# Scores of a 32-head attention laid out with tokens on partitions, one head at a time in two column tiles

## The chip, the cores and the metric

The kernel runs on one core of a Trainium2 chip. The metric is the device time of one execution in microseconds (us); less is better. Five engines work beside each other, each through its own queue of instructions in order: TensorE (PE, matmuls and their weight loads), VectorE (DVE), ScalarE (ACT), GpSimd (POOL) and SyncE (SP, which issues DMAs). They wait for each other by semaphores. Tensors live in SBUF (128 partitions) and matmul results in PSUM banks.

## The reference, cut to what matters

The reference is a decoder of four layers on `x` of 16 x 64 tokens by 512, each an attention with a context and a feed-forward part. The change touches the attention of the second layer only: 32 query heads, 8 key/value heads, head size 128, queries and keys normalised by their root mean square. Every sequence has 64 context tokens and 64 stream tokens, so 128 keys.

```python
kv = jnp.concatenate([context, latents], axis=1)
q = (latents @ Wq).reshape(bsz, q_len, HEADS, HEAD_DIM).transpose(0, 2, 1, 3)
...
q = rms_norm(q, q_norm_w)
k = rms_norm(k, k_norm_w)
qg = q.reshape(bsz, KV_HEADS, groups, q_len, HEAD_DIM)
scale = 1.0 / np.sqrt(HEAD_DIM)
scores = jnp.einsum('bhgqd,bhkd->bhgqk', qg, k) * scale
probs = jax.nn.softmax(scores.astype(jnp.float32), axis=-1).astype(q.dtype)
out = jnp.einsum('bhgqk,bhkd->bhgqd', probs, v)
```

The factor that `rms_norm` gives a query is one number for each token and head. It can be multiplied into the query, or into that query's row of scores later.

## The kernel before

All arithmetic of this attention is fp32. The 1024 tokens are eight tiles of 128 (two sequences of 64 each). A unit is one key/value head with its four query heads (G = 4) on one token tile: 8 heads x 8 tiles = 64 units, two tiles at a time.

Two lanes of work share the core. Lane a runs this attention (`normed_attention`); beside it lane b runs the first layer (window attention with VectorE products, an int8 feed-forward), and then the later parts for half of the tokens. `merged` writes one order of instructions from both by hand: each step of lane a yields a cost, and lane b advances until its own costs have used that up. For PE that order is kept as written (`manual_schedule`, line 1680); the order on the other engines is left to the framework. Each lane has four PSUM banks that it takes in rotation.

Inside lane a `ticks` (line 206) runs the units as a software pipeline. In each tick, in this order: `scores` of the unit begun two ticks ago, `scale` of one tick ago, `project` of five, `queries` of this one, `turn` of one ago, `keys_values` of this one, `values` of four, `turn_weights` of three.

The steps of one unit, with the lines that matter:

- `queries` (838): loads of the context's keys and values from DRAM, the query product (line 857) into a bank, squares into `sq` (865), a copy to SBUF as `qn` (867); tokens are on the partitions, the four heads side by side.
- `keys_values` (870): key and value product (875), square of the keys (883), copies; then `factors`: one sum over `sq` for four query heads and the key (798), a small scaling (799) and a power of -1/2 on POOL (123) give `r`, 128 x 5.
- `scale` (893): DVE multiplies `qn` by its four factors (898, 128 x 512) and `kn` by the fifth (899, 128 x 128), placed behind the latest maximum on DVE's queue (`issue_after(at.last)`).
- `turn` (901): PE transposes the four query blocks (line 141, `ps_qT`), ACT copies them to `qT` with the sequence ahead of the head (905); PE transposes the keys (`ps_kT`) and ACT writes them with the norm weights `nqk` as its scale (909).
- `scores` (914) calls `Attention.weights` (666), which the last layer uses too: four matmuls, each with the 64 tokens of two heads as 128 stationary columns against the 128 keys of their sequence (672). Partitions are therefore (head, token) pairs, and the four blocks are two sequences by two pairs of heads. DVE takes the row maxima (682) and scales them (683); ACT takes four exponentials with the maximum as bias and sums the rows as it goes (688); DVE inverts the sums (696), and POOL multiplies (697).
- `turn_weights` (919): four transposes on PE (`ps_pT`), copied by DVE to `pT` (704).
- `values` (923): two matmuls, values stationary, 256 columns of `pT` moving (713); ACT copies to `aT` (927).
- `project` (930): four matmuls of 512 columns (722), and the residual add on DVE (157).

On PE the score block mostly stands between the transposes `ps_pT` and the projection `ps_wo`. Two other places have blocks of 128 rows by 64 stationary columns: the values' projection of the third layer's attention (line 1110, its last tile) and this attention's context keys (line 809).

Of the kernel before, what the change touches and what calls it, by code (L numbers as in the profile page):

```python
# [8 lines left out]
F32 = mybir.dt.float32  # L9
# [4 lines left out]
AF = mybir.ActivationFunctionType  # L14
ALU = mybir.AluOpType
AX = mybir.AxisListType

P = 128
B, S, D = 16, 64, 512
NTOK = B * S  # L20
NT = NTOK // P
NC = D // P
# [7 lines left out]
def bc(ap, axis, n):  # L30

    a = ap.unsqueeze(axis)
    shape = list(a.shape)
    shape[axis] = n
    return a.to_broadcast(shape)
# [14 lines left out]
VECTOR = mybir.EngineType.DVE  # L50
# [605 lines left out]
class Attention:  # L656


    G = 4
# [6 lines left out]
    def weights(self, qT, kTs):  # L666
# [30 lines left out]
        nc.gpsimd.tensor_tensor(p, p, bc(sm, 2, P), ALU.mult)  # L697
        return p

    def turned(self, p):  # L700

        ps = self.ln.transposed(p.rearrange("p i n -> p (i n)"), 4, "ps_pT")
        pT = self.pool.tile([P, 2, 2 * P], F32, tag="pT", name="pT")
        self.nc.vector.tensor_copy(  # L704
            pT.rearrange("p b n -> p (b n)"), ps.rearrange("p i n -> p (i n)")
        )
        return pT
# [20 lines left out]
def normed_attention(ln, groups, rates, w_in, w_kv, norms):  # L728
# [5 lines left out]
    k, nc = ln.k, ln.nc  # L734
    HD, NKV = 128, 8
    with ExitStack() as es:
        wpool = ln.pool(es, "l1w")
        pool = ln.pool(es, "l1a")
        at = Attention(ln, pool, HD)
        G = at.G  # L740
        nw = pool.tile([P, 2], F32, tag="nw", name="nw", bufs=1)
        nc.sync.dma_start(nw, norms)

        nqk = pool.tile([P, 1], F32, tag="nqk", name="nqk", bufs=1)
        nc.vector.tensor_tensor(nqk, nw[:, 0:1], nw[:, 1:2], ALU.mult)
        NQ, NKVW = NC * G * HD, NC * 2 * HD
        w_qkv, w_o, kept = {}, {}, {}

        def qkv_weights(n):
            if n < NKV * len(groups) and n not in w_qkv:  # L750
                w = wpool.tile([P, NQ + NKVW], F32, tag="qkv", name=f"l1a_w{n}")
                nc.sync.dma_start(w, w_in[n % NKV, :, : NQ + NKVW])
                w_qkv[n] = (
                    w[:, :NQ].rearrange("p (c n) -> p c n", c=NC),
                    w[:, NQ:].rearrange("p (c n) -> p c n", c=NC),
                )

        def out_weights(n):
            if n >= 0 and n not in w_o:
                w = wpool.tile([P, G * D], F32, tag="o", name=f"l1a_o{n}")  # L760
                nc.sync.dma_start(w, w_in[n % NKV, :, NQ + NKVW :])
                w_o[n] = w.rearrange("p (g n) -> p g n", g=G)

        def queries(u):
            n, t = u
            if t == groups[n // NKV][0]:
                qkv_weights(n)
                qkv_weights(n + 1)
                out_weights(n - 2)
            ps = ln.bank([P, G, HD], "ps_q")  # L770
            for c in range(NC):
                nc.tensor.matmul(
                    ps,
                    lhsT=k.stream(c, t),
                    rhs=w_qkv[n][0][:, c, :],
                    start=c == 0,
                    stop=c == NC - 1,
                )
            sq = pool.tile([P, 6, HD], F32, tag="sq", name="sq", bufs=1)
            nc.scalar.activation(sq[:, 0:4, :], ps, AF.Square)  # L780
            qn = pool.tile([P, G, HD], F32, tag="qn", name="qn")
            nc.scalar.copy(qn, ps)
            kept[u] = dict(sq=sq, qn=qn)

        dram = es.enter_context(
            ln.tc.tile_pool(name="saved", bufs=1, space=bass.MemoryType.DRAM)
# [106 lines left out]
        def scale(u):  # L893

            d = kept[u]
            qn, kn, r = d["qn"], d["kn"], d.pop("r")
            with ln.tc.issue_after(at.last) if at.last is not None else ExitStack():
                nc.vector.tensor_tensor(qn, qn, bc(r[:, 0:G], 2, HD), ALU.mult)
                nc.vector.tensor_scalar_mul(kn, kn, r[:, G : G + 1])

        def turn(u):
            d = kept[u]
            ps = ln.transposed(d.pop("qn").rearrange("p g d -> p (g d)"), G, "ps_qT")
            qT = pool.tile([P, 2, G, S], F32, tag="qT", name="qT")
            nc.scalar.copy(
                qT.rearrange("p b g s -> p g b s"), ps.rearrange("p g (b s) -> p g b s", b=2)
            )
            ps = ln.transposed(d.pop("kn"), 1, "ps_kT")
            nc.scalar.mul(
                d["kT"][:, 1:3, :], ps.rearrange("p c (b s) -> p (c b) s", b=2), nqk  # L910
            )
            d["qT"] = qT

        def scores(u):
            d = kept[u]
            kT = d.pop("kT")
            d["p"] = at.weights(d.pop("qT"), [kT[:, 1 - j : 4 - j : 2, :] for j in range(2)])

        def turn_weights(u):
            d = kept[u]  # L920
# [1 line left out]

        def values(u):
            d = kept[u]
            ps = at.values(d.pop("pT"), d.pop("v"))
            aT = pool.tile([P, G, 2, S], F32, tag="aT", name="aT")
            nc.scalar.copy(aT.rearrange("p g b s -> p b g s"), ps)  # L927
            d["aT"] = aT

        def project(u):  # L930
# [13 lines left out]
            [(NKV * i + h, t) for i, ts in enumerate(groups) for h in range(NKV) for t in ts],  # L944
            [
                (2, scores, 0.9),
                (1, scale, 0.0),
                (5, project, 3.4),
                (0, queries, 3.4),
                (1, turn, 0.7),  # L950
                (0, keys_values, 1.7),
                (4, values, 0.9),
                (3, turn_weights, 0.4),
            ],
# [650 lines left out]
def decoder_kernel(ctx: ExitStack, tc: tile.TileContext, i: dict, out: bass.AP):  # L1605
# [64 lines left out]
    def main():  # L1670
        yield Need(0, 1.0)
        yield from normed_attention(
            a, groups, [0.85, 0.78, 0.78, 0.74], i["l1a_w"], i["l1a_kv"], i["l1a_n"]
        )
        yield Need(len(groups) + 2, 1.0)
        a.pages(ctx)
        yield from mxfp4_ffn(a, halves[1], None, i["l1f_b"], kept_w)
        yield from last_layers(a, halves[1])
# [92 lines left out]
```

## Time and profile before

| what | value |
|---|---|
| median of 3 runs | 1642.59 us (1637.8 to 1644.62) |
| span of the profiled execution | 1642.0 us, 0.6 below that median |
| granted TensorE clock, mean | 0.993 |
| score matmuls of the 64 units (line 672, 128 x 128) | 512 records, 275 ns each, 67.8 us of PE busy |
| weight loads of these | 512 records, 192 ns each |
| multiply of the queries by their factors (line 898) | 64 x 683 ns on DVE |
| exponentials (line 688, all callers) | 384 x 369 ns on ACT |
| transposed queries' copy (line 905) | 64 x 604 ns on ACT |

The profiled execution's time is its span, from the first instruction to the last; it is near the median of the runs, so sums made against the span hold for the runs. In the views below a group of instructions is named by line, engine, operation and "out<-in", with tile shapes; "128*64 128x128" is a matmul with 128 rows by 64 columns of weights and a moving operand of 128 partitions by 128 elements. A matmul's record lasts longer than it holds PE, since matmuls are pipelined; what one costs is read from the start of one record to the start of the next. PEld are the weight loads, which overlap matmuls.

### The profile page before, as it was taken

How to read it: one execution, taken by the hardware profiler on the slowest of the kernel's cores; microseconds unless marked ns; L12 is line 12 of the kernel's file. 1: busy time of each engine (PE TensorE's matmuls, PEld its weight loads, DVE VectorE, ACT ScalarE, POOL GpSimd, SP SyncE). 2: the span in 40 equal slices, each digit the busy share in tenths (PEclk: the TensorE clock that was granted, in tenths of full speed). 3: DMA queues.
4: the chain of work that ended last, by engine and by line, in shares of the span. 5: the costliest groups of instructions: out<-in, count | busy, mean ns of one | idle time of the engine just before them, and what ended most of it. 6: DMA issues, size and time to landing. Idle time of an engine off the chain costs nothing.

```text
span 1642.0 us, 20849 instructions
## 1 busy us (share of the span) xinstructions
PE 1590.8 (97%) x7104; PEld 918.9 (56%) x7104; DVE 962.6 (59%) x2000; ACT 614.7 (37%) x1929; POOL 506.2 (31%) x523
## 2 busy tenths in 40 slices
PE   7999899899999999999999999999999999999999
PEld 1334456465555645666655565554566566556774
DVE  6686588566687567776964365338246333522335
ACT  3333354334443444434443454221244332223442
POOL 1493238522385313853322132012022101011112
PEclk9999999999999999999999999999999999999999
DMA  8982359523693346943633222022220101301120
GB/s 259 272 261 82 109 164 257 177 87 120 190 279 118 109 139 176 271 162 107 231 119 126 102 74 97 29 109 73 72 71 20 46 20 49 96 29 42 39 71 26
DMA packets 98329, 200.32 MB, mean 122 GB/s; under 512 B 48945, under 2 KB 66097, under 8 KB 86449
## 3 DMA queue, kind: packets, MB, share of 16 engines
q1 hardware_dynamic: 98224, 199.00, 39.1%
q8 instruction: 57, 0.93, 0.2%
q14 instruction: 48, 0.39, 0.1%
HBM read 179.57 MB, written 19.40 MB: 121 GB/s over the span
## 4 chain that ended last, share of the span: by engine, by line
PE 80%; DVE 10%; DMA 4%; ACT 3%; POOL 2%; issue 1%; SPq 0%; ACTq 0%; POOLq 0%; DVEq 0%
PE ps_wo L722 15%; PE ps_q L857 10%; PE ps_ckv L809 7%; PE ps_kv L875 5%; PE ps_q L1462 5%; PE ps_s L672 4%; PE ps_a L713 4%; PE ps_o L1313 3%; PE ps_h L1288 3%; PE ps_pT L141 3%; DMA att<-att_d 3%; PE ps_v L1409 3%; PE ps_k L1446 2%; PE ps_dot L390 2%; PE ps_wo L1203 2%; PE ps_q L1135 2%
## 5 line engine op out<-in xcount | busy, mean ns | idle before, releaser
L722 PE MATMUL ps_wo<-l1a_o,aT 128*128 128x512 f32 x512 | 231.1, 594 | 3.1 <-ACT aT L927 3.1
L857 PE MATMUL ps_q<-l1a_w,kvT 128*128 128x512 f32 x512 | 233.0, 598 | 0.0
L688 ACT ACTIVATE p<-ps_s,mx 128x128 f32<-128x128 f32 x384 | 135.4, 369 | 211.2 <-DVE mx L683 192.4
L697 POOL TENSOR_TENSOR p<-p,sm 128x512 f32<-128x512 f32 x96 | 103.7, 1080 | 337.3 <-DVE sm L696 303.0
L123 POOL TENSOR_TENSOR r<-r,mhalf 128x5 f32<-128x5 f32 (+1 forms) x96 | 102.9, 1072 | 294.6 <-DVE r L799 280.4
L857 PEld LDWEIGHTS ps_q<-l1a_w,kvT 128*128 128x128 f32 x512 | 96.4, 192 | 117.5 <-issue 116.1
L722 PEld LDWEIGHTS ps_wo<-l1a_o,aT 128*128 128x128 f32 x512 | 92.7, 190 | 100.8 <-issue 96.3
L157 DVE TENSOR_TENSOR x<-x,ps_wo 128x512 f32<-128x512 f32 x104 | 70.6, 679 | 115.2 <-PE ps_wo L722 83.0
L875 PE MATMUL ps_kv<-l1a_w,kvT 128*128 128x256 f32 x512 | 125.0, 388 | 1.1 <-DVE x L157 0.9
L476 POOL TENSOR_TENSOR acc<-acc,pv 128x512 f32<-128x512 f32 x96 | 122.0, 1295 | 4.7 <-DVE pv L466 4.0
L809 PE MATMUL ps_ckv<-l1a_kv,kvT 128*64 128x512 f32 x512 | 116.9, 599 | 0.0
L798 DVE TENSOR_REDUCE r<-sq 128x5 f32<-128x640 f32 x64 | 52.3, 817 | 109.9 <-ACT sq L883 109.9
L123 POOL TENSOR_TENSOR rs<-rs,mhalf 128x1 f32<-128x1 f32 x64 | 36.7, 578 | 259.1 <-DVE rs L132 225.1
L875 PEld LDWEIGHTS ps_kv<-l1a_w,kvT 128*128 128x128 f32 x512 | 94.2, 194 | 18.6 <-issue 4.2
L865 ACT ACTIVATE sq<-ps_q 128x512 f32<-128x512 f32 x64 | 38.2, 597 | 158.3 <-PE ps_q L857 158.2
L466 DVE TENSOR_TENSOR pv<-att,ps_v 128x512 f32<-128x512 f32 x128 | 82.1, 676 | 22.1 <-DMA att<-att_d 18.8
L672 PE MATMUL ps_s<-kT,qT 128*128 128x128 f32 (+1 forms) x704 | 92.1, 276 | 0.1
L369 DVE TENSOR_TENSOR prod<-qs,kp 128x1024 f32<-128x1024 f32 x64 | 79.0, 1272 | 15.4 <-ACT qs L350 7.4
L704 DVE COPY pT<-ps_pT 128x512 f32<-128x512 f32 x96 | 64.3, 683 | 39.3 <-PE ps_pT L141 39.2
L672 PEld LDWEIGHTS ps_s<-kT,qT 128*128 128x128 f32 (+1 forms) x704 | 85.0, 192 | 3.4 <-issue 2.1
L1462 PE MATMUL ps_q<-kvT,l3a_w 128*128 128x256 f32 x384 | 85.6, 379 | 0.0
L722 PE MATMUL ps_wo<-l3a_o,aP 128*128 128x512 f32 x192 | 85.5, 593 | 0.0
(193 smaller groups left out, 2720.8 us busy)
## 6 DMA issues: line engine op xcount, KB each, us to landing
l1a_w<-in_l1a_w SPq DMA_DIRECT2D x32, 1536.0 KB, 7.0
att<-att_d SPq DMA_DIRECT2D x64, 512.0 KB, 9.2
l1a_o<-in_l1a_w SPq DMA_DIRECT2D x32, 1024.0 KB, 5.2
s<-ckv SPq DMA_DIRECT2D x32, 256.0 KB, 3.9
l3a_w<-in_l3a_w SPq DMA_DIRECT2D x6, 1024.0 KB, 5.2
l3a_o<-in_l3a_w SPq DMA_DIRECT2D x8, 768.0 KB, 4.3
l1a_kv<-in_l1a_kv SPq DMA_DIRECT2D x4, 1024.0 KB, 7.2
dots_d<-dots SPq DMA_DIRECT2D x16, 256.0 KB, 2.0
```

The costliest lines, as they stand in the source:

```text
L123: self.nc.gpsimd.tensor_tensor(out, v, self.k.mhalf[:, : v.shape[1]], ALU.pow)
L369: nc.vector.tensor_tensor(prod, bc(qs, 1, 2), spaced(kp, b * NB + j + 2 * w, [[2, 2], [1, D]]), ALU.mult,)
L466: nc.vector.tensor_tensor(pv.rearrange("p (q w n) -> p q w n", w=2, n=L), att[:, a, :].rearrange("p (q w n) -> p q w n", w=2, n=L), spaced ...
L476: nc.gpsimd.tensor_tensor(sums, before, pv, ALU.add)
L672: nc.tensor.matmul(ps[:, i, :], lhsT=qT[:, i // 2, 2 * (i % 2) : 2 * (i % 2) + 2, :].rearrange("p g s -> p (g s)"), rhs=kTs[i // 2], start ...
L688: nc.scalar.activation(p[:, i, :], ps[:, i, :], AF.Exp, bias=mx[:, i : i + 1], scale=self.scale, accum_out=sm[:, i : i + 1],)
L697: nc.gpsimd.tensor_tensor(p, p, bc(sm, 2, P), ALU.mult)
L722: self.nc.tensor.matmul(ps, lhsT=a, rhs=wo[:, g, :], start=g == 0, stop=g == len(chunks) - 1)
L809: nc.tensor.matmul(ps[j * S : (j + 1) * S], lhsT=k.context(c, 2 * t + 1 - j), rhs=w_pair[hp][:, c, :], start=c == 0, stop=c == NC - 1,)
L857: nc.tensor.matmul(ps, lhsT=k.stream(c, t), rhs=w_qkv[n][0][:, c, :], start=c == 0, stop=c == NC - 1,)
L875: nc.tensor.matmul(ps, lhsT=k.stream(c, t), rhs=w_qkv[n][1][:, c, :], start=c == 0, stop=c == NC - 1,)
L1462: nc.tensor.matmul(ps[:, j], lhsT=wq[:, c, (j0 + j) * P : (j0 + j + 1) * P], rhs=k.kvT[:, c, t : t + 2, 1:3, :], start=c == 0, stop=c == N ...
```

## The change

A new method takes the place of `Attention.weights` in this attention alone. Scores are computed per head: for each of the four heads and each of the two sequences one matmul with that sequence's 64 query columns, writing to partitions 0 to 63 or 64 to 127. A partition is then a token, and the four blocks are the four heads. The query's factor is thus a column of the partition and enters as the scale of the exponential; the maximum is multiplied by it and by -1. The multiply of `qn` by its factors is gone. The constant `HD**-0.5` moves into `nqk`. `qT` is copied in the order in which the transposes lie. `values` is written out, since the order of the weights' columns is another: 256 moving columns are now four pieces of 64. An unused first definition of `queries`, which a later one of that name replaced, is deleted as well.

```diff
+    def weights_by_token(self, qT, kTs, r):
+        nc, ln, G = self.nc, self.ln, self.G
+        ps = ln.bank([P, G, P], "ps_s")
+        for g in range(G):
+            for b in range(2):
+                rows = slice(b * S, (b + 1) * S)
+                nc.tensor.matmul(
+                    ps[rows, g, :], lhsT=qT[:, g, rows], rhs=kTs[b], start=True, stop=True
+                )
+        mx = ln.small.tile([P, G], F32, tag="mx", name="mx")
+        nc.vector.tensor_reduce(mx, ps, AX.X, ALU.max)
+        nc.vector.scalar_tensor_tensor(mx, mx, -1.0, r, ALU.mult, ALU.mult)
+        self.last = ln.last_of(VECTOR)
+        p = self.pool.tile([P, G, P], F32, tag="p", name="p", bufs=2)
+        sm = ln.small.tile([P, G], F32, tag="sm", name="sm")
+        for g in range(G):
+            nc.scalar.activation(
+                p[:, g, :],
+                ps[:, g, :],
+                AF.Exp,
+                bias=mx[:, g : g + 1],
+                scale=r[:, g : g + 1],
+                accum_out=sm[:, g : g + 1],
+            )
+        nc.vector.reciprocal(sm, sm)
+        nc.gpsimd.tensor_tensor(p, p, bc(sm, 2, P), ALU.mult)
+        return p
...
-        nc.vector.tensor_tensor(nqk, nw[:, 0:1], nw[:, 1:2], ALU.mult)
+        nc.vector.scalar_tensor_tensor(
+            nqk, nw[:, 0:1], HD**-0.5, nw[:, 1:2], ALU.mult, ALU.mult
+        )
...
-            qn, kn, r = d["qn"], d["kn"], d.pop("r")
+            kn = d["kn"]
             with ln.tc.issue_after(at.last) if at.last is not None else ExitStack():
-                nc.vector.tensor_tensor(qn, qn, bc(r[:, 0:G], 2, HD), ALU.mult)
-                nc.vector.tensor_scalar_mul(kn, kn, r[:, G : G + 1])
+                nc.vector.tensor_scalar_mul(kn, kn, d["r"][:, G : G + 1])
...
-            qT = pool.tile([P, 2, G, S], F32, tag="qT", name="qT")
-            nc.scalar.copy(
-                qT.rearrange("p b g s -> p g b s"), ps.rearrange("p g (b s) -> p g b s", b=2)
-            )
+            qT = pool.tile([P, G, P], F32, tag="qT", name="qT")
+            nc.scalar.copy(qT, ps)
...
-            d["p"] = at.weights(d.pop("qT"), [kT[:, 1 - j : 4 - j : 2, :] for j in range(2)])
+            d["p"] = at.weights_by_token(
+                d.pop("qT"), [kT[:, 1 - j : 4 - j : 2, :] for j in range(2)], d.pop("r")[:, :G]
+            )
...
-            ps = at.values(d.pop("pT"), d.pop("v"))
+            pT = d.pop("pT").rearrange("p a n -> p (a n)").rearrange("p (g n) -> p g n", g=G)
+            ps = ln.bank([P, 2, G, S], "ps_a")
+            for j in range(2):
+                nc.tensor.matmul(
+                    ps[:, j],
+                    lhsT=d["v"][:, j, :],
+                    rhs=pT[:, :, j * S : (j + 1) * S],
+                    start=True,
+                    stop=True,
+                )
+            d.pop("v")
```

More of the change, by code (lines that the diff above doesn't have):

```diff
@@ L762, in out_weights @@
                 w_o[n] = w.rearrange("p (g n) -> p g n", g=G)
[L764 to L777, printed above, removed]
-                )
[L779 to L783, printed above, removed]
         dram = es.enter_context(
@@ L903, in turn @@
             ps = ln.transposed(d.pop("qn").rearrange("p g d -> p (g d)"), G, "ps_qT")
-            qT = pool.tile([P, 2, G, S], F32, tag="qT", name="qT")
-            nc.scalar.copy(
-                qT.rearrange("p b g s -> p g b s"), ps.rearrange("p g (b s) -> p g b s", b=2)
-            )
+            qT = pool.tile([P, G, P], F32, tag="qT", name="qT")
+            nc.scalar.copy(qT, ps)
             ps = ln.transposed(d.pop("kn"), 1, "ps_kT")
```

## The prediction

> **What bounds the kernel now.** I read the page's busy line, its slices and its chain first, then the busy time of the stage that the change touches, then that stage's waits, and last TensorE's timeline.
>
> ```profile
> PE 1590.8 (97%) x7104; PEld 918.9 (56%) x7104; DVE 962.6 (59%) x2000; ACT 614.7 (37%) x1929; POOL 506.2 (31%) x523
> ...
> PE   7999899899999999999999999999999999999999
> ...
> PE 80%; DVE 10%; DMA 4%; ACT 3%; POOL 2%; issue 1%; SPq 0%; ACTq 0%; POOLq 0%; DVEq 0%
> ```
>
> TensorE (PE) is busy 97% of the 1642.0 us span, and 80% of the chain that ended last is PE. The 64 units of the 32-head attention run from about 185 to 1106 us:
>
> ```profile
> 185.00:1106.00 921.00, 900.66 (x4024) 538.24 (x4022) 606.90 (x1227) 379.62 (x1232) 341.65 (x328) 0.99 0.48 147
> ```
>
> The columns are length, then busy PE, PE weight loads, VectorE (DVE), ScalarE (ACT), GpSimd (POOL). PE idles 921.0 - 900.7 = 20.3 us of this stage; DVE is at 66%. PE's order is written by hand, so what PE gains or loses per unit moves the end one for one, and no other engine can give back more than those 20 us. The view of PE's waits in this stage sums to 19.3 us, with these lines among them:
>
> ```profile
> PE ps_qT L141 <- DVE qn L898: 4.6, 3, 2.1
> PE ps_gu L596 <- POOL qT L573: 3.9, 2, 2.1
> PE ps_wo L722 <- ACT aT L927: 2.4, 2, 2.2
> PE ps_kT L141 <- ACT p L688: 0.6, 2, 0.3
> ```
>
> Columns: total us, times, longest. Only the first is a wait for what the change removes.
>
> **The change, part by part.**
>
> *1. The scores on PE.* Before, four matmuls per unit: 128 stationary columns (two heads by 64 tokens), 128 moving columns. Each fp32 matmul shows as two records, so a unit has 8. After: eight matmuls with 64 stationary columns, writing partitions 0-63 and 64-127 in turn, so 16 records on two column tiles. Neighbours in PE's timeline of today, start and length in us:
>
> ```profile
> 569.56 1.03 PE L713 MATMUL ps_a<-pT,v 128*128 128x256 f32 x4
> 570.43 0.60 PE L141 MATMUL ps_pT<-ident,p 128*128 128x128 f32 x4
> 570.87 1.06 PE L672 MATMUL ps_s<-kT,qT 128*128 128x128 f32 x8
> 571.76 3.60 PE L722 MATMUL ps_wo<-l1a_o,aT 128*128 128x512 f32 x8
> 575.20 0.60 PE L141 MATMUL ps_xT<-ident,xn 128*128 128x128 f32 x4
> ```
>
> Lengths overlap (matmuls are pipelined), so I use start to start: scores hold PE 571.76 - 570.87 = 0.89 us, the projection 3.44, a value product 0.87. Another layer already has exactly the new form, 16 records of 128 rows by 64 columns against 128 moving columns, alternating between the two halves of the partitions:
>
> ```profile
> 891.00 1.03 PE L713 MATMUL ps_a<-pT,v 128*128 128x256 f32 x4
> 891.96 1.09 PE L1110 MATMUL ps_v<-w_l2k,kvT 128*64 128x128 f32 x16
> 892.99 0.66 PE L141 MATMUL ps_pT<-ident,p 128*128 128x128 f32 x4
> ```
>
> and a projection stands right behind another tiled block (line 390, 32 columns):
>
> ```profile
> 224.56 3.70 PE L722 MATMUL ps_wo<-l1a_o,aT 128*128 128x512 f32 x8
> 228.10 1.45 PE L857 MATMUL ps_q<-l1a_w,kvT 128*128 128x512 f32 x3
> ```
>
> The two halves do run side by side: 16 records start within 0.82 us, against 0.78 for the 8 full ones. So the streaming is a draw. The borders are not. Into the tiled block: 891.96 - 891.00 = 0.96 instead of 0.87, +0.09. The block with its way out: 1.03 instead of 0.89, +0.14. In the first product behind it the second record starts 0.10 later: 228.10 - 224.56 = 3.54 instead of 3.44. Together +0.33 us per unit, 64 x 0.33 = 21.1. In the timeline of all units, 59 score blocks come after ps_pT and 49 before ps_wo; two now follow a tiled block and four precede one, where a border is paid today already (-1.2 us together), and three precede transposes, whose first interval grows by 0.056 instead of 0.10 (-0.15). **Term: +19.7 us, all on PE.** Bounds from these rows: 17 (the way out counted half) to 21.
>
> [...]
>
> *2. The query multiply goes from DVE.*
>
> ```profile
> L898 DVE TENSOR_TENSOR qn<-qn,r x64: 668/683/1830, 185.8 to 1068.8; 128x512 f32<-128x512 f32 x64
> ```
>
> 64 x 0.683 = 43.7 us of DVE, hidden today except in the 4.6 us of PE waits above. The query transposes then need only ACT's copy of a tick earlier. Late next are the key transposes behind them, which need kn: they start 0.43 us later (566.85 to 567.29 in the timeline), and kn, no longer queued behind qn, is done 0.68 - 0.28 = 0.40 earlier than qn was. That takes 0.83 from each of the three waits at once, 2.5 us, and up to 4.6 if the shorter queue brings DVE nearer to its work. Much of the freed DVE time stays idle: in most units DVE goes on to sm (line 696), which waits for the exponentials anyway (22.3 us of such waits in 185:1080). I take 4.5 us back on PE; bounds 0 and 19.3 (every wait).
>
> *3. The exponential's scale is now a column r.* 4 x 64 exponentials on ACT. No row has an exponential with two columns; the rows nearest:
>
> ```profile
> L688 ACT ACTIVATE p<-ps_s,mx 128x128 f32<-128x128 f32 x384 | 135.4, 369 | 211.2 <-DVE mx L683 192.4 <-DVE sc L564 8.0 <-issue 5.6
> ...
> L909 ACT ACTIVATE kT<-ps_kT,nqk 128x128 f32<-128x128 f32 x64 | 25.2, 394 | 0.0
> ...
> L883 ACT ACTIVATE sq<-ps_kv 128x128 f32<-128x128 f32 x64 | 17.8, 279 | 48.1 <-PE ps_kv L875 47.6
> ```
>
> No column: 279 ns; bias column: 369; scale column: 394. So one more column costs between 0 and 115 ns; I take 90, by the step from 279 to 369, the same size. That is 256 x 0.09 = 23 us on ACT (41% busy here, 380 of 921), and 0.36 us per unit between maximum and weights. Cover: the weights are transposed a tick later (in the stretch above, p was done at 575.9 and wanted at 583.3), and the bank of the scores is wanted again by ps_kT, a median of 3.7 us after the last exponential. The shortest gaps are 0.1 to 0.5 us, in about 1 unit in 20; there PE will wait longer: 4 units x 0.25, +1 us; bounds 0 and +5. If the cover were gone everywhere: 64 x 0.36 = +23.
>
> [...]
>
> *4. Parts that cost nothing on the path.* The maximum's scaling becomes a scalar_tensor_tensor on 128x4: today 219 ns (line 683); another operand, 0 to 0.1 us, I take 0.03, on DVE inside the same cover as part 3. It now waits for r, which POOL made a tick before; behind it on DVE queue kn, sm and the residual add, but the wait is over before the scores are there. nqk: one small instruction at 9 us. ACT's copy of qT is contiguous (604 ns now; 586 for the like-sized aT copy): -1 us on ACT. The value product reads its moving operand in four pieces of 64 instead of 256 in a row: line 672 reads in pieces of 64 today and keeps the 0.112 us between records that line 1110's full form has contiguous, so 0. r lives until the exponentials, two ticks, with four buffers: no new wait. No DMA moves. PE gets 512 more matmul records and as many loads, already in part 1.
>
> **Sum.** +19.7 (scores) - 4.5 (waits for qn) + 1.0 (banks, exponentials) = +16.2 on the span of 1642.0: 1658.2. The median run, 1642.59, is 0.6 above that span: **1659 us.**
>
> **Rivals.**
> *a. The waits come back.* A lighter DVE and a slower PE let the other lane catch up (ps_gu waiting for POOL, ps_wo for ACT). If 15 of the 19.3 us go: 1642.6 + 19.7 + 1 - 15 = 1648. For it: the waits are few and up to 2.3 us, signs of backlog. Against: most wait for POOL and ACT, which get no lighter.
> *b. Faster: DVE is the stage's real bound.* The place is ps_qT and all that follows from a late DVE; the price is the 19.3 us of waits; it decides if the tiled block costs under (19.3 - 8.2)/64 = 0.17 us per unit, half of what the rows show, as when its borders fell into waits. With borders free (0.04 x 64 = 2.6) and 12 us back: 1633. Against: 97.8% busy PE in the stage.
> *c. The weights arrive late.* The exponentials' 0.36 us reach PE through ps_kT and ps_pT in most units: 1642.6 + 19.7 + about 13 = 1675. Against: gaps of a median 3.7 us or more.
> *d. The change does not do what it says:* the two column halves run one after another, 16 x 0.11 = 1.76 us, +0.93 per unit, 60 more: 1718. Against: line 1110's starts.
>
> **Chances.** Forecast 0.73 (own range 1651 to 1667), a 0.13, b 0.03, c 0.08, d 0.03. Anything within 0.5% (8.2 us, about what a measurement can tell from no change) is under 1650.8: rival a. Faster 0.03, same 0.13, slower 0.84. The range 1647 to 1668 leaves out b, c, d and a part of a.
>
> **What would show it.** Score blocks of 16 records with about 1.03 us to the next product's start; 0.09 before them; the following projection at 3.54; PE's waits for qn gone; exponentials at 460 ns; DVE some 40 us lighter with longer waits at sm; PE records 7616; everything before 185 us unchanged and after the attention merely shifted. Wrong: borders that cost nothing, or PE idle in the stage far from 16 us.

## The result, and the profile after

The changed kernel took 1650.7 us (median of 9 runs, 1647.8 to 1658.2) against 1639.6 for the kernel before (9 runs of the same job): **1.0059 times, interval 1.0038 to 1.0080**, or +9.7 us (6.2 to 13.1). The forecast was 1659, or 16.4 us more than the 1642.6 known then. The direction and the place were right; the size was not.

One execution's time is its span and about 1.85 us around it. The profiled execution of before, span 1642.0, thus took about 1643.9, some 4 us above that kernel's later median, and its granted clock was 0.993 where the mean over all its runs was 0.995. The forecast counted from this execution. The profile of after has a span of 1649.1 us, a clock of 0.996, and a time of 1650.95, at its median. The same page lines as those shown of before, now of after:

```profile
PE 1604.4 (97%) x7611; PEld 916.6 (56%) x7616; DVE 929.1 (56%) x1936; ACT 638.4 (39%) x1929; POOL 506.9 (31%) x523
...
PE   7999899899999999999999999999999999999999
...
PE 86%; DVE 6%; ACT 3%; DMA 2%; POOL 2%; issue 2%; SPq 0%; ACTq 0%; POOLq 0%; DVEq 0%
```

PE is busy 13.6 us longer and has 512 more weight loads; it is 86% of the chain instead of 80%. DVE is busy 33.5 us less, ACT 23.7 us more. The timeline of PE in the same stretch (start, length, as before):

```profile
570.42 0.60 PE L141 MATMUL ps_pT<-ident,p 128*128 128x128 f32 x4
570.95 1.09 PE L708 MATMUL ps_s<-kT,qT 128*64 128x128 f32 x16
571.97 3.70 PE L752 MATMUL ps_wo<-l1a_o,aT 128*128 128x512 f32 x8
575.51 0.60 PE L141 MATMUL ps_xT<-ident,xn 128*128 128x128 f32 x4
```

The block's start to the projection's start is 1.02 us (predicted 1.03, before 0.89), and the projection holds PE for 3.54 us (predicted 3.54, before 3.44). As medians over all units: the way in from `ps_pT` is 202 ns from record to record (before 109), the 16 records lie within 822 ns (8 records in 782), the way out is 203 ns (112), and the next product's first interval 533 ns (432).

The waits of PE in the stage (185 to 1113 us; total, times, longest) sum to 12.9 us, where they were 19.3:

```profile
PE ps_gu L596 <- POOL qT L573: 3.4, 2, 2.2
PE ps_wo L752 <- ACT aT L947: 2.3, 2, 2.1
...
PE ps_kv L886 <- ACT p L718: 0.9, 1, 0.9
...
PE ps_kT L141 <- ACT p L718: 0.2, 1, 0.2
```

The wait for `qn` is gone, as predicted, and other, smaller ones went with it.

**A balance of PE.** I took all intervals from the start of one PE record to the start of the next, from the first score block to the last projection of the attention (917.6 us before, 924.8 after), sorted them by what stands at their two ends, and compared the two profiles:

| intervals | after minus before, us |
|---|---|
| into, inside and out of the score blocks, and the first interval of the next product | +21.5, of which 2.25 is a wait of `ps_gu` that now falls right behind a score block: borders **+19.2** |
| to the query transposes (`ps_qT`), where PE waited for `qn` | **-5.1** |
| all the rest, with that `ps_gu` wait | **-6.9** |
| sum | +7.2 |

The tiled blocks cost what the prediction said (19.7), and the wait for `qn` gave about what it said (4.5). What it had at nothing is the third line. Before's profile was 4 us high, so of the 12.0 us given back about 8 remain against a median run; by the timed ratio it is 19.7 - 9.7 = 10. That is the question for the experiments.

**Theory 1:** VectorE lost its multiplies (64 x 683 ns = 44 us by the median, 53.9 us by the sum of their records), everything behind it in its queue comes earlier, and this takes PE's waits away. **Theory 2:** each PE wait is a race that another engine loses by little; with a slower PE they arrive in time whatever the work is that slows it, and VectorE's relief matters little. **Theory 3,** a rival to both: the tiled blocks cost less in the whole than at their borders, or the price is not at the borders.

### The profile page after: what moved, and what is told of

Read it like the earlier page. It is cut to its first block, busy times and chain, and to the rows that moved or that the text cites. A ratio compares the mean times of both kernels' runs of the same rounds, so it can differ in the third digit from the quotient of the medians.

```text
span 1649.1 us, 21814 instructions
## 1 busy us (share of the span) xinstructions
PE 1604.4 (97%) x7611; PEld 916.6 (56%) x7616; DVE 929.1 (56%) x1936; ACT 638.4 (39%) x1929; POOL 506.9 (31%) x523
## 4 chain that ended last, share of the span: by engine, by line
PE 86%; DVE 6%; ACT 3%; DMA 2%; POOL 2%; issue 2%; SPq 0%; ACTq 0%; POOLq 0%; DVEq 0%
PE ps_wo L752 16%; PE ps_q L868 11%; PE ps_ckv L820 7%; PE ps_kv L886 6%; PE ps_q L1482 5%; PE ps_o L1333 3%; PE ps_s L708 3%; PE ps_h L1308 3%; PE ps_pT L141 3%; PE ps_a L938 3%; PE ps_v L1429 3%; PE ps_k L1466 2%; DMA att<-att_d 2%; PE ps_s L672 2%; PE ps_dot L390 2%; PE ps_gu L596 2%
## 5 line engine op out<-in xcount | busy, mean ns | idle before, releaser
L752 PE MATMUL ps_wo<-l1a_o,aT 128*128 128x512 f32 x512 | 235.9, 603 | 3.0 <-ACT aT L947 3.0
L718 ACT ACTIVATE p<-ps_s,mx,r 128x128 f32<-128x128 f32 x256 | 113.9, 454 | 188.8 <-DVE mx L713 166.6
L1482 PEld LDWEIGHTS ps_q<-kvT,l3a_w 128*128 128x128 f32 x384 | 72.1, 190 | 11.7 <-issue 2.4
```

What stands on the lines that cost most here:

```text
L718: nc.scalar.activation(p[:, g, :], ps[:, g, :], AF.Exp, bias=mx[:, g : g + 1], scale=r[:, g : g + 1], accum_out=sm[:, g : g + 1],)
L752: self.nc.tensor.matmul(ps, lhsT=a, rhs=wo[:, g, :], start=g == 0, stop=g == len(chunks) - 1)
L1482: nc.tensor.matmul(ps[:, j], lhsT=wq[:, c, (j0 + j) * P : (j0 + j + 1) * P], rhs=k.kvT[:, c, t : t + 2, 1:3, :], start=c == 0, stop=c == N ...
```

## The experiments

Ratios are against before in the same job, where its median was 1639.3 to 1639.9 us. The trace of a run is of one execution, whose time can lie several us off the median of its kernel.

### tiles_only and plain_scale: the parts of the change taken back

`tiles_only` is the changed kernel with the multiply of the queries back on VectorE and a constant scale on the exponentials; `plain_scale` has the constant scale, but no multiply, and so leaves out the query norm. Both have, against after:

```diff
-        nc.vector.scalar_tensor_tensor(mx, mx, -1.0, r, ALU.mult, ALU.mult)
+        nc.vector.tensor_scalar_mul(mx, mx, -1.0)
...
-                scale=r[:, g : g + 1],
+                scale=1.0,
```

and `tiles_only` also

```diff
+                nc.vector.tensor_tensor(
+                    d["qn"], d["qn"], bc(d["r"][:, 0:G], 2, HD), ALU.mult
+                )
```

> The changed kernel with the VectorE multiply of the queries put back and constant scales in the exponentials: the column tiles alone. Theory 1 (the borders of the tiled block cost their full 0.31 us per unit, and it is the lighter VectorE that gave back about 9 us): +18 to +20 us over the kernel before, waits of TensorE for qn as before (4 to 5 us). Theory 2 (a slower TensorE lets the other engines catch up, so the borders fall into waits by themselves): +10 to +13 us, about the time of the changed kernel.

> The changed kernel with a constant as the exponential's scale and the maximum scaled by -1; it leaves out the queries' normalisation. It takes away the second column operand of 256 exponentials (454 ns each now) and nothing else. Both theories: exponentials back at 367 ns, time within 1 us of the changed kernel, since the weights are wanted a tick later. If the longer exponentials do reach TensorE: 3 us or more faster than the changed kernel.

`tiles_only`: 1649.04 us, **1.0063** (1.0041 to 1.0084), or +10.3 us (6.7 to 13.8). With the multiply kept, the cost is the same as with the whole change within the intervals, and the 18 to 20 us of theory 1 are outside; so the relief of VectorE isn't what gave the time back. In its waits of PE (185 to 1113), 12.5 us in all, the wait for VectorE's `qn` is down to 0.3 us, once, though `qn` is still multiplied:

```profile
PE ps_gu L596 <- POOL qT L573: 3.5, 2, 1.7
PE ps_wo L752 <- ACT aT L950: 2.6, 3, 1.7
...
PE ps_kv L886 <- DVE x L157: 1.2, 4, 0.5
...
PE ps_qT L141 <- DVE qn L909: 0.3, 1, 0.3
```

By the balance, its borders are +18.6, the way to `ps_qT` -4.2, the rest -9.7: the same picture, without any relief.

`plain_scale`: 1648.69 us, 1.0062 (1.0038 to 1.0086), within the interval of after. Its exponentials take 366 ns, those of after 454:

```profile
L718 ACT ACTIVATE p<-ps_s,mx 128x128 f32<-128x128 f32 x256 | 90.7, 366 | 189.4 <-DVE mx L713 167.6 <-DVE sc L564 7.7 <-PE ps_q L868 3.7
```

The 23 us of ScalarE that the scale column costs do not show in the time.

### no_multiply: the relief alone

Before, without its multiply (and so without the query norm):

```diff
-                nc.vector.tensor_tensor(qn, qn, bc(r[:, 0:G], 2, HD), ALU.mult)
```

> The kernel before without the VectorE multiply of the queries by their factors; it leaves out the queries' normalisation. It shows what the 43.7 us of VectorE are worth on TensorE without any tiles. Theory 1: 7 to 9 us faster than before. Theory 2: 1 to 4 us faster. The forecast's own term was 4.5 us.

1641.07 us (12 runs), **1.0004** (0.9987 to 1.0021): leaving out every multiply gains at most 2.1 us. Here theory 1 falls; of the 1 to 4 us of theory 2 only the low end is left. The profile (waits of PE, 185 to 1106, 19.0 us in all) shows why the gain does not come:

```profile
PE ps_gu L596 <- POOL qT L573: 4.3, 2, 2.2
PE ps_kT L141 <- ACT p L688: 3.3, 2, 2.3
PE ps_wo L722 <- ACT aT L926: 3.1, 3, 2.2
```

The wait for `qn` (4.6 us before) is gone, and 3.3 us stand at the key transposes right behind, for a bank that the exponentials still hold. Before, this line had 0.6 us. One profile alone would have misled: its span is 1636.5, 5.5 below that of before, where the timed runs show no gain. What it shows of single waits is of an execution 2.8 us under its kernel's median.

### three_more_transposes: a slower PE with other work

Before, with three more transposes of the weights in each unit, into a block that is written anyway. It adds no borders, does not touch the multiply or the exponentials, and costs 3 x 64 x 0.109 = 20.9 us of PE.

```diff
-    def turned(self, p):
+    def turned(self, p, extra=0):
...
+        flat = p.rearrange("p i n -> p (i n)")
+        ps = self.ln.transposed(flat, 4, "ps_pT")
+        for _ in range(extra):
+            self.nc.tensor.transpose(ps[:, 3, :], flat[:, 3 * P : 4 * P], self.ln.k.ident)
...
-            d["pT"] = at.turned(d.pop("p"))
+            d["pT"] = at.turned(d.pop("p"), 3)
```

> The kernel before with three more transposes of 0.109 us in each unit (a block of the weights transposed again to the same place): 64 x 0.327 = 20.9 us of TensorE work, about what the borders cost, in one tiling mode throughout and with VectorE's multiply kept. Theory 2 (TensorE work added evenly to the units is partly paid out of waits that vanish, and out of the half-clock stretches behind such waits, whatever the work is): +11 to +13 us over the kernel before, mean clock 0.996 or more. Rival (what came back is particular to column tiles or to their borders): +19 to +21 us, clock as before (0.995).

1655.29 us, **1.0090** (1.0074 to 1.0105): +14.8 us (12.1 to 17.2) for 20.9 of work. About 6 us come back with nothing made lighter, and the waits of PE in the stage are 12.6 us instead of 19.3, with no wait of `ps_qT` left, though its multiply is there. This trace is of the fastest of the six runs (1649.28), 6 us under their median, so it is the times that size what came back. The longest two waits:

```profile
PE ps_gu L596 <- POOL qT L573: 4.6, 2, 3.6
PE ps_wo L725 <- ACT aT L930: 1.8, 2, 1.1
```

The rival's 19 to 21 us are outside the interval; theory 2 had 11 to 13, and the median is above that. Its other sign, a mean clock of 0.996 or more, did not come: it is 0.995 over the six runs, as in before and after. So theory 2 holds in kind: part of PE's added work is paid out of waits whatever the work is. The sum of PE's waits from 185 to 1113 us points the same way over the traces: 20.0 us in before, 15.0 and 18.4 with about 10 us of added borders (`first_half` and `second_half`, below), 12.5 to 14.3 with about 20 of work (after, `tiles_only`, `plain_scale` and this run), 8.1 with about 50 (`one_half_first`, below). What stays unsettled is the amount: the change gave back about 10 us (6.6 to 13.5) for 19.7, this 6.1 (3.7 to 8.8) for 20.9. The intervals overlap.

### multiply_on_pool: the relief paid elsewhere

Before, with the multiply on GpSimd:

```diff
-                nc.vector.tensor_tensor(qn, qn, bc(r[:, 0:G], 2, HD), ALU.mult)
+                nc.gpsimd.tensor_tensor(qn, qn, bc(r[:, 0:G], 2, HD), ALU.mult)
```

> The kernel before with the multiply of the queries moved from VectorE to GpSimd, right behind the power that makes the factors; no tiles, nothing left out. GpSimd gets 64 x 1.04 us (by its 128x512 multiply of line 697) at 37% busy in the stage. Theory 1: VectorE's relief counts, 4 to 8 us faster than before. Theory 2: within 2 us of before. Slower if GpSimd's later finish (0.36 us more per multiply, and the work queued behind it) reaches the transposes.

1650.81 us, 1.0063 (1.0041 to 1.0085), which is the "slower" of what was expected and neither theory's number. It cannot separate the theories as cleanly as meant: POOL takes 1079 ns for each multiply, and VectorE's key multiply beside it grows from a mean of 318 to 682 ns.

```profile
L898 POOL TENSOR_TENSOR qn<-qn,r 128x512 f32<-128x512 f32 x64 | 69.1, 1079 | 4.7
```

PE's waits from 185 to 1113 us are 22.0 us against 20.0. The trace is of the fastest of the six runs (1645.4), so where most of the 10 us went is not shown. The place of the queries' factors is not free on every engine; on the scale of the exponential it showed no cost (`plain_scale`).

### one_half_first: the halves in the other order

After, with the sequence outside and the head inside, so that four matmuls go to one column half and then four to the other:

```diff
-        for g in range(G):
-            for b in range(2):
+        for b in range(2):
+            for g in range(G):
```

> The changed kernel with the loops over heads and sequences exchanged: the four matmuls of the lower partitions first, then the four of the upper. If two column tiles run side by side only where neighbours in the queue use different halves: 16 records take up to 1.76 us instead of 0.82, up to 60 us more than the changed kernel. If the queue looks far enough ahead: no change.

One run: 1670.1 us, span 1668.2. The block of 16 records now takes 1309 ns in the median instead of 822:

```profile
574.33 1.58 PE L708 MATMUL ps_s<-kT,qT 128*64 128x128 f32 x16
575.84 3.70 PE L752 MATMUL ps_wo<-l1a_o,aT 128*128 128x512 f32 x8
```

From 574.33 to 575.84 it is 1.51 us against 1.02. So in these two orders the halves overlap well where neighbours in the queue are on different halves, and about half as well where they are not (1309 ns, between the 822 and an estimated 15 x 0.111 = 1.67 us with no overlap, by the 111 ns from record to record in line 1110's full form); the order written in the change is what keeps rival d away. Of 64 x 0.487 = 31 us of raw cost 19 reach the span (1668.2 - 1649.1): again a part of PE's added work is swallowed, and PE's waits are down to 8.1 us.

### half_the_borders and its controls: is the price at the borders?

After, with the score blocks of two units back to back at every second tick, so that the stage has 134 changes between full-size (128 x 128) and smaller weight tiles instead of 196 (before: 80), and the same order on the kernel before as `pairs_without_tiles`:

```diff
+        waiting = []
+        def scores_of_two(u):
+            waiting.append(u)
+            if len(waiting) < 2:
+                return 0.0
+            for w in waiting:
+                scores(w)
+            waiting.clear()
+            return 1.8
...
-                (2, scores, 0.9),
+                (2, scores_of_two, 0.9),
```

> The changed kernel with the scores of two units back to back, every second tick: the same matmuls, 32 tiled blocks instead of 64, so 32 x 0.31 = 9.9 us less at the borders. Theory 2 (the price sits at the borders, and some of it is paid out of waits): 5 to 9 us less than the changed kernel, 1641 to 1645 us. Rival (the price sits in the 64-column matmuls themselves): no change from the changed kernel, 1650 us.

> The kernel before with the scores of two units back to back, every second tick: the control for the reordering in half_the_borders, no tiles. All theories: within 3 us of the kernel before; what it differs by is the reordering's own part.

`half_the_borders` 1648.48 us, 1.0059 (1.0047 to 1.0071); `pairs_without_tiles` 1645.13, 1.0029 (1.0018 to 1.0040). As it stands this is the rival's outcome: the ratio is that of the changed kernel, and the 5 to 9 us did not come. Only against its own control does the tiled form cost less, 3.4 us by the medians (4.9 by the ratios, about 2 to 8 if the two intervals are put together) with 54 added borders, where the change costs 11.1 (9.7, 6.2 to 13.1) with 116. These intervals overlap, so the times alone do not decide it. The traces do: 32 records of a doubled block lie within 1695 ns (16 full ones in the control: 1675), with one way in (203 ns) and one way out (202) for two units, and the balance of `half_the_borders` against its control has +8.2 us at the 32 blocks, where the change has +19.2 at 64. The price on PE goes with the borders, and theory 3 falls by the balances. But the pairs cost about as much as they save, where the control was expected within 3 us of before; its waits, in a trace 3.4 us under its median, show one place:

```profile
PE ps_wo L722 <- ACT aT L927: 8.9, 27, 0.9
```

In every tick without a score block nothing stands between the value product and the projection, and PE waits for ACT's copy of `aT`. I tried to fill that place with the query product (`queries` ahead of `project` in the tick), on both and on before alone:

```diff
+                (0, queries, 3.4),
                 (5, project, 3.4),
-                (0, queries, 3.4),
```

> The kernel before with the query product ahead of the projection in each tick; no tiles, nothing else. It puts 3.4 us between the value product and the projection that needs its copy. Control for the two runs beside it: within 3 us of the kernel before.

> pairs_without_tiles with the query product ahead of the projection. If the 5.4 us that pairing cost were the waits of the projection for aT (27 waits, 8.9 us in its trace): those waits go and the time is within 2 us of the kernel before. If pairing costs in another way: 1644 to 1646 us as there.

> half_the_borders with the query product ahead of the projection: 32 borders pairs without the waits for aT. If the price sits at the borders (9.9 us of raw work for 32, some of it paid out of waits): 2 to 6 us over pairs_queries_first, 1641 to 1646 us, 5 to 9 us less than the changed kernel. If half the borders cost as much as all: 1648 to 1651 us. No theory has it below the kernel before.

This did not help, and all three came out slower than any number expected for them: `queries_first` 1644.17 us, 1.0026 (1.0009 to 1.0043); `pairs_queries_first` 1649.48, 1.0057 (1.0037 to 1.0076); `half_the_borders_queries_first` 1653.45, 1.0083 (1.0063 to 1.0103). Most of the waits for `aT` went (8.9 to 1.2 us), others came in their place (25.4 us of waits from 185 to 1113 us in `pairs_queries_first`, 8.9 of them of `ps_a` for VectorE's residual add, the largest line). Tiled against untiled it is again 4.0 us by the medians with half the borders, though here the two intervals put together reach from about 0 to 9. No version was faster than before.

### first_half and second_half: where in the stage?

The whole change in the first 32 units only, or in the last 32 only; the other units keep the form of before.

```diff
+        def by_token(u):
+            return u[0] < 2 * NKV
```

(`>=` in the second.)

> The whole change for the first 32 units alone (score blocks before about 630 us, beside the window attention), the other 32 as before. 31 or 32 tiled blocks, 9.9 us of raw border cost. Theory (in this part TensorE waits for VectorE, GpSimd and the loads anyway, and the borders fall into these waits and into the half-clock stretches behind them): 0 to +3 us over the kernel before. Rival (what came back is spread over all units): +4 to +6 us.

> The whole change for the last 32 units alone (score blocks from about 630 us on, beside layers that TensorE bounds), the first 32 as before. The same 9.9 us of raw border cost. Theory: nearly all of it is paid, +7 to +10 us over the kernel before. Rival (spread over all units): +4 to +6 us.

`first_half` 1644.12 us, 1.0028 (1.0011 to 1.0045); `second_half` 1646.85, 1.0053 (1.0033 to 1.0072). The first 32 units run beside the window attention of lane b, where PE waits most. In the windows of the two halves of the stage (length, then busy PE, PEld, DVE, ACT, POOL), before:

```profile
185.00:630.00 445.00, 432.72 (x1856) 252.73 (x1855) 310.91 (x570) 189.79 (x621) 186.55 (x181) 0.99 0.54 157
630.00:1106.00 476.00, 467.94 (x2170) 285.51 (x2169) 296.00 (x658) 189.82 (x612) 155.10 (x147) 1.00 0.42 137
```

and after:

```profile
185.00:630.00 445.00, 437.31 (x2105) 250.34 (x2104) 295.96 (x535) 200.62 (x619) 186.64 (x181) 0.99 0.52 157
630.00:1106.00 476.00, 470.27 (x2414) 282.51 (x2416) 274.89 (x622) 201.63 (x612) 154.86 (x147) 1.00 0.42 137
```

Before, PE idles 12.3 us in the first part and 8.1 in the second; after, 7.7 and 5.7. From the 33rd score block to the last projection it is 479.7 us before and 485.7 after: 6.0 of 9.9 us of borders remain. The clock is not at half anywhere in this second part, and the other runs repeat it: `first_half` 479.6, `second_half` 485.7 (a trace 4 us above its kernel's median), `tiles_only` 487.2, and `three_more_transposes` 487.4 (7.7 of its 10.5 us).

From the first score block to the 33rd it is 437.9 and 439.1, which looks as if 1.2 of 9.9 remained. But before's trace has three stretches of half the clock there and after's two (see the end). At an estimated 1.7 us for each, the first part is 432.8 before against 435.7 after, and the other traces agree: 431.5 to 433.8 in `no_multiply`, `multiply_on_pool` and `second_half`, where it is untiled, 434.7 to 435.9 in `first_half`, `tiles_only` and `plain_scale`, where it is tiled. So about 3 of 9.9 us remain in the first part and 6 in the second, 9 together, near the 9.7 that was timed.

The timed runs point the same way (+4.6 and +8.7 us by the ratios), but +4.6 is what the rival had for the first half, above the theory's 0 to 3, and the intervals (1.8 to 7.4 and 5.4 to 11.8) overlap; by the times alone an even split stays possible.

## Why the prediction was off, step by step

- **The scores on PE, +19.7: right.** Each border came out as read from line 1110 and line 390, and the balance has +19.2 on PE. The halves run side by side (822 ns, predicted 0.82 us), and the block got no shorter (782 before).
- **"I take 4.5 us back on PE; bounds 0 and 19.3": this is the step that failed, by its size and by its reason,** and with it the premise that "what PE gains or loses per unit moves the end one for one". 20.9 us of plain transposes moved the end by 14.8 (12.1 to 17.2), and the 19.7 of the tiles by 9.7 (6.2 to 13.1). The waits for `qn` did go, and gave 5.1. But they also went in `tiles_only` (4.6 to 0.3) and `three_more_transposes` (to nothing), where `qn` is still multiplied, and their going alone gained nothing in `no_multiply`. The term should have been headed "PE gets slower", not "VectorE gets lighter", and it is 19.7 + 1.0 - 9.7 = 11 us by the timed ratio (7.6 to 14.5), inside its bounds of 0 and 19.3.
- **Rival a had the mechanism.** It was set at 0.13 on the argument "most wait for POOL and ACT, which get no lighter". They need not get lighter: 20.9 us of transposes that relieve nobody took the waits from 19.3 to 12.6. The time lies between the forecast (1659) and the rival (1648), nearer the rival.
- **Exponentials, +1.0: right in kind.** They take 454 ns (predicted 460), ACT grew by 23.7 us (predicted 23). PE's waits for `p` in the stage are 1.1 us after, 0.6 before; `plain_scale` shows no gain outside the interval.
- **The parts at nothing** were nothing on the path, but two readings of VectorE were off. The 64 x 683 ns of the query multiply is a median; its records sum to 53.9 us, a mean of 842 ns, since ten of the 64 took over 800 ns (up to 1830). And the key multiply, of unchanged form, went from a mean of 318 to 464 ns, 9.4 us in all, though its median only went from 278 to 286. The two lines in before, then that of the keys in after, with the exponentials:

```profile
L898 DVE TENSOR_TENSOR qn<-qn,r 128x512 f32<-128x512 f32 x64 | 53.9, 842 | 6.4 <-POOL r L123 6.4
```

```profile
L899 DVE TENSOR_SCALAR kn<-kn,r 128x128 f32<-128x128 f32 x64 | 20.3, 318 | 0.0
```

```profile
L718 ACT ACTIVATE p<-ps_s,mx,r 128x128 f32<-128x128 f32 x256 | 113.9, 454 | 188.8 <-DVE mx L713 166.6 <-PE ps_q L868 7.7 <-DVE sc L561 5.4
...
L909 DVE TENSOR_SCALAR kn<-kn,r 128x128 f32<-128x128 f32 x64 | 29.7, 464 | 8.4 <-POOL r L123 8.4
```

  The long ones changed hands. In after 13 key multiplies take over 400 ns (up to 1364), in before three. All 13, and all ten long query multiplies of before, lie beside an instruction on GpSimd, mostly `acc<-acc,pv`; of the 51 short ones of after nine do. Without the multiply ahead of them the keys take 464 to 483 ns in the mean (after, `no_multiply`, `plain_scale`), with it 318 to 355 (before, `tiles_only`, `three_more_transposes`). So it goes with what stands first behind the factors, not with the tiles; that GpSimd is the cause was not tried.

- **VectorE's freed time idles, as said:** its waits at the inverted sums (line 696, now 726) for the exponentials rose from 22.3 to 50.1 us in the stage.
- **The base.** 1642.6 was the median of three runs; later ones give 1639.6. Of the 8.3 us between 1659 and 1650.7, 3.0 are this, and 5.3 the failed term by the medians (by the ratio, +16.4 against +9.7, it is 6.7).
- **Rival b** needed borders under 0.17 us; they cost 0.30 to 0.33. **Rival c** did not come: the waits for `p` are 1.1 us. **Rival d** did not come with this order of the loops, and half came with the other.
- Idle PE from 185 to 1110 us is 925.0 - 911.6 = 13.4 us, against the "16" that the prediction named as its test.

**What stays open.** The change's 10 us and the transposes' 6 differ by less than their intervals. Part of the balance's -6.9 is the clock of these two executions (below); the rest is many small intervals. Over all timed runs the mean clock is 0.995 in before and after alike, so the clock does not explain the timed difference.

## What to carry to other kernels

When an engine that is busy 97% gets x us of new work, do not add x: look at the waits that it still has. Here they were 20.0 us from 185 to 1113 us, the longest 2.2, and fell to 12.5 to 14.3 with about 20 us of added work of two kinds, tiles and plain transposes; 6 to 10 us of 20 came back, by the traces more of it where waits were dense. The same held backward: taking away the named releaser of a wait showed no gain in time in `no_multiply` (1.0004, 0.9987 to 1.0021), where 4.6 us of waits for `qn` went and 3.3 us stood at the key transposes right behind. A tiled block's price was at its borders here (+19.2 us at 64 blocks, +8.2 at 32), so count the changes of form, not the rows; and keep a copy of the same order without the change as a control, or the order's own cost is booked to the wrong side.

## What the runs showed of the hardware

**Stretches of half the clock stand beside short idle gaps of TensorE.** In the records of the granted clock, stretches of 0.5 come in multiples of 3.4 us (3.41 or 6.83 us each in before and in after). In before, PE waited 2.0 us for `qn` up to 303.6 us and 1.5 us for POOL's `acc` up to 307.3; the clock is at half from 305.9 to 312.7, and the window of 300 to 316 us has a mean of 0.79:

```profile
300.00:316.00 16.00, 12.27 (x50) 6.38 (x49) 8.65 (x17) 4.65 (x17) 4.12 (x4) 0.79 0.27 86
```

The same window of `tiles_only`, with no such gap and 74 records instead of 50:

```profile
300.00:316.00 16.00, 16.00 (x74) 8.57 (x73) 10.30 (x29) 4.95 (x19) 6.29 (x6) 1.00 0.43 141
```

In the 15 profiles there are 52 such stretches ahead of the end. 51 of them began within 2.9 us, before or after, of the end of a PE gap of 1.29 us or more; the other followed two gaps of 0.90 and 0.87 us close together. Of 83 gaps of 1.4 to 2.9 us, 37 had such a stretch (24 of the 38 from 2.0 us on), and so had all 15 gaps of 5.0 us, one in each profile at about 170 us. Each stretch of 3.4 us costs up to an estimated 1.7 us (3.4 at half speed, with PE busy in it). So a wait of 2 us with one such stretch beside it goes with a loss of nearly 4 by this estimate, and before's profile had three such stretches in the attention (two of them in a row), after's two: an estimated 1.7 of the 6.9 us in the balance. The runs of before spread from 1632.2 us (mean clock 0.997) to 1646.3 (0.991) in one job of 23 runs, and the longer ones have mostly the lower mean clock. That links the spread to these stretches, but no run changed the gaps alone, so neither is shown to be their cause.

**Borders of a tiled fp32 block** (64 stationary columns, alternating halves) cost 93 ns on the way in (109 to 202), 91 on the way out (112 to 203), and 101 in the first interval of a 512-wide product behind it (432 to 533), besides 40 ns inside (782 to 822). **The order inside the block** matters more than the borders here: 1309 ns against 822 for the same 16 records.

**A second column operand** on an exponential of 128 x 128 cost 454 - 366 = 88 ns (after against `plain_scale`).
